# Normalizing the first twelve tiles on ScalarE and reading a wave of outputs back later, in a two-layer graph and expert network on one core

## The chip, the cores and the metric

One core of a Trainium2 chip runs the whole program in one launch. The core has TensorE (PE, matrix products; its weight loads are PEld), VectorE (DVE), ScalarE (ACT), GpSimd (POOL) and SyncE (SP), which here issues most of the transfers. The metric is the device time of one execution, in microseconds (us); lower is better.

## The reference, cut to what matters

3327 nodes have 256 features each. There are two layers, and each has a graph step and a step of eight experts, of which every node uses two.

```python
# layer 0
x = x + relu(adj @ (layernorm(x) @ W) + b)
x = x + moe0(layernorm(x))        # 8 experts, top 2, 256 -> 1024 -> 256, relu
# layer 1
a = tanh(adj * adj) where adj > 0  # top 700 of a row are kept
h2 = tanh(layernorm(x) @ W_proj + b_proj)
x = x + relu(a @ (h2 @ W_gcn) + b_gcn)
t = layernorm(x)
x = x + t + moe1(t)               # 8 experts, top 2, 256 -> 256 -> 256, gelu
```

`layernorm` subtracts a row's mean and divides by the root of its variance plus 1e-5. All is fp32.

## The kernel before

The nodes are padded to 3328, which gives 26 tiles of 128 rows. `x` holds all tiles in SBUF for the whole run, and `s` holds the right-hand operand of the graph product. The adjacency matrix comes in 13 panels of 256 columns, each in two chunks of 13 tiles (1664 KB); six ring buffers (`ring0` to `ring5`) take the chunks in turn, and the experts' weights later on. A tile framework records the program: it puts each instruction into the queue of its engine in a fixed order and sets the semaphore waits from the accesses it has recorded. `issue_after` and the helper `behind` move an instruction behind another one in that order.

**The start.** The loads of tokens and of the first chunk of panels 0 and 1 go out on SP in slices (line 147): for each of four groups of tiles, (0, 2), (2, 2), (4, 4) and (8, 5), the tokens, then panel 0's slice, then panel 1's; then the tokens of the last thirteen tiles. POOL meanwhile builds constants and issues six small transfers (`gnn_b_sb`, `f0_bg_sb`, `g1_wg_sb`, `f1_r_sb`, `f1_b1_sb`, `g1_bp_sb`; 1 to 256 KB). PE runs 54 short products on constants ahead of the first real one.

Line 1111 normalizes the tiles in groups: (0, 2), (2, 2), (4, 4), (8, 4), (12, 6), (18, 8). `statistics` (line 267) computes mean and variance on DVE, two instructions a tile, and the reciprocal root by three steps of Newton's method, in small dependent instructions. `layernorm` (line 290) then writes each tile of `s` with one DVE instruction, `(x - mean) * rs` (line 297). The first product, `aggregate_first` (line 371), takes the tiles j of the first chunk in order, and for each j first panel 0 and then panel 1 (line 424, `add`, line 383). Then it goes panel by panel. The bias `gnn_b_sb` is first read when panel 0 is finished (line 329). ScalarE counts the positive entries of each piece with Sign (line 1126); a ring buffer is loaded again when PE and these counts have read it.

**The end.** In layer 1 the experts work on blocks of tokens; `step` does one block. Its `second` (line 954) ends in `scatter` (line 551), an indirect transfer on POOL that writes the weighted outputs to rows of `ys1` in DRAM. The last six blocks hold 128 rows (one scatter), the others 256 (two). The outputs are read back from `ys1` with `load_outputs` (line 1050, issued by SP), added to `x` by `add_loaded` (line 1064, two DVE instructions for one read), and `x` is written to the result.

This read-back comes in three parts. Tiles 0 to 13 are the first wave: seven reads of two tiles (512 KB), one after each block from the 18th, each added two blocks later, with the write to the result (line 1384, ScalarE's queue) a block after that. Tiles 14 to 21 are the second wave: four reads of two tiles, after the 27th to the 30th of the 32 blocks. Tiles 22 to 25 are read one by one (256 KB) behind the last block. The loop adds only the first wave; the second one and the last four tiles are added in `with behind(last_y)` (line 1409), behind the last block's DVE work, and written by ScalarE's queue, two of them by SP's (line 1413). The list `written` holds the scatters that a wave must wait for; besides, the framework lets a read wait for the newest scatter that is recorded ahead of it. All loads of blocks are issued by SP ahead of the first read of the second wave.

Of the kernel before, what the change touches and what calls it, by code (L numbers as in the profile page):

```python
# [22 lines left out]
P = 128  # L23
NT = 26
# [67 lines left out]
def gnn_moe_two_layers(  # L92
# [41 lines left out]
    def piece(pan, k):  # L134
        return ring[(pan * NCHUNK + k) % RING].rearrange("p (c w) -> p c w", w=PW)
# [8 lines left out]
        gates.append(g)  # L144
        return d

    for t, n in [(0, 2), (2, 2), (4, 4), (8, CJ - 8), (CJ, NT - CJ)]:
        nc.sync.dma_start(out=x[:, t : t + n, :], in_=x_in[:, t : t + n, :])
        if t < CJ:
            for pan in range(2):  # L150
                nc.sync.dma_start(
                    out=piece(pan, 0)[:, t : t + n, :], in_=adjT[pan, 0, :, t : t + n, :]
                )

    ones_sq = const.tile([P, P], BF16, name="ones_sq")
    nc.gpsimd.memset(ones_sq, 1.0)
# [74 lines left out]
    def behind(instructions):  # L231

        if instructions and any(i is instructions[-1].ins for i in nc.cur_bb.bb.instructions):
            return tc.issue_after(instructions[-1].ins)
        return nullcontext()
# [7 lines left out]
    def on_all_partitions(name, b):  # L243
        t = const.tile([P, b.shape[1]], F32, name=name)
        nc.gpsimd.dma_start(out=t, in_=b.partition_broadcast(P))
        return t
# [3 lines left out]
        nc.gpsimd.dma_start(out=t, in_=a)  # L250
        return t

    gnn_b_sb = on_all_partitions("gnn_b_sb", g0_b[0:1, :])
    f0_bg_sb = on_all_partitions("f0_bg_sb", f0_bg[0:1, :])
    gate = state.tile([P, E, D], F32, name="gate")

# [114 lines left out]
    def aggregate_first(b_sb, w, w_sb, begin, count, after):  # L371

        sums, waiting, copied = {}, [], []

        def start(pan):
            sums[pan] = [psy.tile([P, PW], F32, name="ps_g", tag="py") for _ in range(DC)]

        def add(pan, j):
            for c in range(DC):
                nc.tensor.matmul(  # L383
                    sums[pan][c],
                    lhsT=s[:, j, ts(c, P)],
                    rhs=piece(pan, j // CJ)[:, j % CJ, :],
                    start=(j == 0),
                    stop=(j == NT - 1),
                )

        def finish():
            pan, g = waiting.pop()
            for it in range(PW // P):
                ps = psh.tile([P, D], F32, name="ps_o", tag="ph")
                for c in range(DC):
                    nc.tensor.matmul(  # L396
                        ps, lhsT=g[:, c, ts(it, P)], rhs=w_sb[:, c, :], start=(c == 0),
                        stop=(c == DC - 1),
                    )
                add_relu(x[:, pan * (PW // P) + it, :], ps, b_sb)  # L400
            after(pan)

        def rest(pan, first):
            for j in range(first, NT):
                add(pan, j)
                if waiting and j == first + BEHIND:
                    finish()
            g = work.tile([P, DC, PW], F32, name="xnT", bufs=2)
            for c in range(DC):
                copied.append(nc.scalar.copy(g[:, c, :], sums[pan][c]))  # L410
            waiting.append((pan, g))

        loaded = RING // NCHUNK
        for pan in range(loaded):
            load_panel(pan, lambda pan, k, a: None, begun=1 if pan < 2 else 0)
            if pan == 1:
                nc.sync.dma_start(out=w_sb, in_=w.rearrange("(c p) n -> p c n", p=P))
                with tc.issue_after(last_piece[0].ins):
                    turn_gate(f0_wgT)
        with tc.issue_after(last_piece[0].ins):  # L420
            turn_gate(f1_rT)
        for pan in range(2):
            start(pan)
        for j in range(CJ):
            for pan in range(2):
                add(pan, j)
        for pan in range(NPAN):
            if pan > 1:
                start(pan)
            if loaded < min(pan + RING // NCHUNK, NPAN):  # L430
                load_panel(loaded, lambda pan, k, a: None)
                loaded += 1
            begin(pan)
            count(pan, copied)
            rest(pan, CJ if pan < 2 else 0)
        return finish
# [648 lines left out]
    def fill(*lists):  # L1085


        with tc.issue_after(last_piece[0].ins):
# [13 lines left out]
            for xlist in lists:  # L1102
                for e in range(E):
                    first = xlist[e * NP : e * NP + SB, :].rearrange("(g p) d -> p g d", p=P)
                    nc.sync.dma_start(out=first[:, :, 0:ID], in_=zeros)
                    with nc.allow_non_contiguous_dma("two elements of a partition"):
                        nc.sync.dma_start(
                            out=first[:, :, ID : ID + 1], in_=rows_f[:, e, :].unsqueeze(2)
                        )

    for t0, n0 in [(0, 2), (2, 2), (4, 4), (8, 4), (12, 6), (18, 8)]:
        with behind(last_normalized if t0 < 12 else ()):
            layernorm(t0, n0, xn=s[:, t0 : t0 + n0, :].unsqueeze(2))

    with tc.issue_after(last_normalized[0].ins):
        g1_wg_sb = by_feature("g1_wg_sb", g1_wg)
        f1_r_sb = by_feature("f1_r_sb", f1_rT)
        f1_b1_sb = plain("f1_b1_sb", f1_b1)
        g1_bp_sb = plain("g1_bp_sb", g1_bp)

    def count(pan, copied):
        for k in range(NCHUNK):
# [225 lines left out]
    with tc.If(first_usual > 0) as arms:  # L1348
        output_loads.clear()
        for yt, t, n in begun:  # L1350
            load_outputs(yt, ys0, t, n, written, "read0")
        layer0.step(late)
        layer0.step(late)
        with behind(last_y):
            add_begun()
        layer0.step(late)
        with behind(last_y):
            statistics(0, BEGUN, begun_stats)
        layer0.steps_to(late, layer0.always)
        between()  # L1360
        layer1 = new_layer1()
        aggregate(gnn_b_sb, filter_chunk, panels1(layer1, True), loaded=ahead)
        late1 = first_blocks(layer1)

        layer1.steps_to(late1, EARLY - 1)
        layer1.step(late1, place=blk.tile([P, DC, SB], F32, name="xT_arms", bufs=1))
        baset, nbt = late1[4], late1[6]  # L1370
        second_usual = usual(
            [(FIRST_TILES, baset[:, E : 2 * E]), (MORE_TILES, baset[:, 2 * E :])],
            [(late1[5][0:1, :], FIXED[1])],
            nbt[:, E : 2 * E],
        )
        before_inner = layer1.state()
        with tc.If(second_usual > 0) as inner:  # L1377
            layer1.know(2 * E)
            waiting, asked, added, k = [], [], [], 0
            while len(layer1.started) < layer1.always:  # L1380
                layer1.step(late1)
                at = len(layer1.started)
                for tiles in added:
                    nc.scalar.dma_start(out=rows_of(out, *tiles), in_=x[:, tiles[0] : sum(tiles), :])
                added.clear()
                if at == EARLY + 2 * E - 2:
                    layer1.know_rest(late1)

                with behind(last_y):
                    if asked and asked[0][2] + 1 < at <= layer1.always - FIXED[1]:  # L1390
                        yt, tiles, _ = asked.pop(0)
                        add_loaded(yt, *tiles)
                        added.append(tiles)
                if waiting and at > waiting[0][1] + (1 if k < FIRST_TILES // 2 else 2):
                    tiles, _, written = waiting.pop(0)
                    yt = ring[k % RING][:, PIECE - 2 * K * D :].rearrange("p (n d) -> p n d", n=2)
                    load_outputs(yt, ys1, *tiles, written, "read1")
                    asked.append((yt, tiles, at))
                    k += 1
                if at in (EARLY + E, EARLY + 2 * E):  # L1400
                    tiles = range(0, FIRST_TILES, 2) if at == EARLY + E else range(FIRST_TILES, MORE_TILES, 2)
                    waiting.extend(((t, 2), at, list(outputs)) for t in tiles)
            assert not (waiting or added)
            left = []
            for i, t in enumerate(range(MORE_TILES, NT)):
                yt = ring[i][:, 0 : K * D].rearrange("p (n d) -> p n d", n=1)
                load_outputs(yt, ys1, t, 1, outputs)
                left.append((yt, (t, 1)))
            with behind(last_y):
                for i, (yt, tiles) in enumerate([(yt, tiles) for yt, tiles, _ in asked] + left):  # L1410
                    add_loaded(yt, *tiles)
                    queue = nc.sync if i > len(asked) and i % 2 else nc.scalar
                    queue.dma_start(out=rows_of(out, *tiles), in_=x[:, tiles[0] : sum(tiles), :])
        with inner.Else():
            layer1.back_to(before_inner)
            layer1.rest(late1)
            finish(FOURS)
# [168 lines left out]
```

## Time and profile before

| what | value |
|---|---|
| median of 4 runs | 1235.65 us |
| lowest and highest of them | 1230.36 and 1237.18 us |
| the profiled execution | 1230.29 us |
| its span in the profile | 1228.6 us |
| PE busy | 1188.8 us, 97% of the span |
| DVE, ACT, POOL busy | 707.4, 511.9 and 270.4 us |
| granted clock of PE | 0.994 of full speed |
| moved by DMA | 241.59 MB, mean 197 GB/s |

The span runs from the first to the last instruction of the profiled execution. A busy time is the sum of an engine's instructions; issuing a transfer and waiting are not in it. In the timeline a row gives the start and the duration in microseconds, the engine, the line, the operation, what it writes and reads, and in brackets how long its engine sat idle before it and what ended that. "x4" means four instructions in one row, whose duration then runs from the first one's start to the last one's end. SPq, ACTq and POOLq are the queues of those engines, in which transfers are issued. "L297" is line 297 of the kernel.

### The profile page before, as it was taken

To read this page: it belongs to the slowest core of one execution; us is meant where nothing else is said; L and a number is where in the kernel's file an instruction comes from. 1 tells how busy PE (TensorE), PEld (TensorE's weight loads), DVE (VectorE), ACT (ScalarE), POOL (GpSimd) and SP (SyncE) were. 2 spreads that over 40 slices of the span, in tenths; PEclk is the share of its full clock that TensorE was granted. 3 is DMA by queue.
4 is the path that set the end of the run, shared out by engine and by line. 5 is a ranking of instruction groups with operands and counts; after the bars stand their busy time and mean duration, and the time that the engine had idled before them with its cause. 6 is when DMAs were issued, how large, how long until landed. Compare 5 with 4: busy or idle time off the path is not lost. (4 is left out here: it accounts for less than half of the span.)

```text
span 1228.6 us, 18156 instructions
## 1 busy us (share of the span) xinstructions
PE 1188.8 (97%) x5819; PEld 1028.7 (84%) x5819; DVE 707.4 (58%) x2841; ACT 511.9 (42%) x950; POOL 270.4 (22%) x341
## 2 busy tenths in 40 slices
PE   8999999999999999999999999999999999988983
PEld 7888888888888888888888888888888888877872
DVE  7577756766682111211111268479999998776464
ACT  2655456445322222223232235995555552033331
POOL 3004111211241111111111110003224223254541
PEclk9999999999999999999999999999999999999997
DMA  9898744444357556757566647235445542476797
GB/s 340 192 325 259 207 160 154 159 159 138 102 189 251 181 184 188 251 180 252 185 219 224 245 171 286 75 149 201 173 147 195 184 152 79 136 232 186 230 295 229
DMA packets 123177, 241.59 MB, mean 197 GB/s; under 512 B 24480, under 2 KB 93120, under 8 KB 116160
## 3 DMA queue, kind: packets, MB, share of 16 engines
q1 hardware_dynamic: 108656, 205.59, 51.1%
q0 software_dynamic: 11136, 31.60, 7.0%
q10 hardware_dynamic: 3280, 3.15, 0.8%
q8 instruction: 48, 0.79, 0.3%
q14 instruction: 57, 0.47, 0.1%
HBM read 203.98 MB, written 36.33 MB: 196 GB/s over the span
## 5 line engine op out<-in xcount | busy, mean ns | idle before, releaser
L383 PE MATMUL ps_g<-ring,s 128*128 128x256 f32 x1352 | 295.6, 380 | 4.6 <-DVE s L297 4.6
L360 PE MATMUL ps_g<-s,ring 128*128 128x256 f32 x1352 | 294.2, 380 | 0.0
L383 PEld LDWEIGHTS ps_g<-ring,s 128*128 128x128 f32 x1352 | 255.7, 190 | 40.3 <-DVE s L297 6.0
L360 PEld LDWEIGHTS ps_g<-s,ring 128*128 128x128 f32 x1352 | 256.0, 190 | 34.4
L941 PE MATMUL ps_h<-xT,ring 128*128 128x256 f32 (+1 forms) x1176 | 249.3, 365 | 3.8 <-ACT xT L932 3.6
L941 PEld LDWEIGHTS ps_h<-xT,ring 128*128 128x128 f32 x1176 | 204.3, 190 | 41.1 <-ACT xT L932 4.7
L948 ACT ACTIVATE wide<-ps_h,ring 128x256 f32<-128x256 f32 (+1 forms) x240 | 110.3, 460 | 285.1 <-PE ps_h L941 264.8
L447 DVE SCALAR_TENSOR_TENSOR rt_product<-xn,gate 128x256 f32<-128x256 f32 x400 | 198.6, 497 | 12.2
L980 PE MATMUL ps_y<-ring,wide 128*128 128x256 f32 x896 | 200.3, 379 | 0.0
L551 POOL DMA_INDIRECT xlist<-xn,rt_idx x104 | 105.0, 1009 | 392.1 <-DVE ln_ve L278 154.4
L980 PEld LDWEIGHTS ps_y<-ring,wide 128*128 128x128 f32 x896 | 167.1, 190 | 21.0
L1126 ACT ACTIVATE sign<-ring,below 128x416 bf16<-128x416 f32 x208 | 133.5, 642 | 9.3 <-DMA ring<-in_adjT 3.1
L551 POOL DMA_INDIRECT ys<-narrow,index x56 | 54.9, 981 | 326.6 <-DVE narrow L988 234.6
L1275 ACT ACTIVATE ring<-ring 128x3328 f32<-128x3328 f32 x22 | 65.4, 2978 | 87.5 <-DVE ring L1274 50.7
L932 DVE COPY xT<-ptb 128x512 f32<-128x512 f32 (+1 forms) x29 | 18.9, 651 | 142.1 <-PE ptb L929 142.1
L987 DVE TENSOR_TENSOR narrow<-ps_y,ring 128x256 f32<-128x256 f32 x56 | 23.8, 424 | 131.7 <-PE ps_y L980 131.6
L512 ACT ACTIVATE rt_d<-rt_d 128x2 f32<-128x2 f32 x26 | 5.3, 203 | 162.9 <-DVE rt_d L511 162.2
L551 POOL DMA_INDIRECT ys<-wide,index x58 | 57.5, 991 | 62.5 <-DVE wide L988 34.1
L1276 ACT ACTIVATE ring<-ring 128x3328 f32<-128x3328 f32 x22 | 65.4, 2977 | 0.6
L329 DVE TENSOR_TENSOR gnn_t<-ps_o,gnn_b_sb 128x256 f32<-128x256 f32 x26 | 11.0, 424 | 82.8 <-PE ps_o L396 82.8
L980 PE MATMUL ps_y<-s,narrow 128*128 128x256 f32 (+1 forms) x200 | 48.4, 381 | 1.1 <-issue 1.0
L275 DVE BATCH_NORM_STATS2 ln_st<-x 128x6 f32<-128x256 f32 x104 | 42.1, 414 | 5.5 <-DMA x<-in_x 4.9
(213 smaller groups left out, 1035.1 us busy)
## 6 DMA issues: line engine op xcount, KB each, us to landing
ring<-in_adjT SPq DMA_DIRECT2D x50, 1664.0 KB
ring<-in_f_w1T SPq DMA_DIRECT2D x30, 1024.0 KB
ring<-in_f_w2T SPq DMA_DIRECT2D x30, 1024.0 KB
ring<-xlist SPq DMA_DIRECT2D x52, 258.0 KB
ring<-in_f_w SPq DMA_DIRECT2D x36, 256.0 KB
ring<-ys SPq DMA_DIRECT2D x12, 512.0 KB
ring<-in_f_b SPq DMA_DIRECT2D x34, 128.0 KB
xlist<-wide SPq DMA_DIRECT2D x16, 257.0 KB
```

The source lines that it names most:

```text
L275: nc.vector.bn_stats(out=st, in_=x[:, t0 + g, :])
L360: nc.tensor.matmul(ps[it], lhsT=chunks[k][:, c, ts(it, P)], rhs=s[:, j, :], start=(j == 0), stop=(j == NT - 1),)
L383: nc.tensor.matmul(sums[pan][c], lhsT=s[:, j, ts(c, P)], rhs=piece(pan, j // CJ)[:, j % CJ, :], start=(j == 0), stop=(j == NT - 1),)
L447: nc.vector.scalar_tensor_tensor(product, xn[:, g, 0, 0:D], 1.0, gate[:, e, :], ALU.mult, ALU.mult, accum_out=sc[:, g, e : e + 1],)
L551: d = nc.gpsimd.indirect_dma_start(out=a[:, :], out_offset=bass.IndirectOffsetOnAxis(ap=index, axis=0), in_=rows_, in_offset=None,)
L941: nc.tensor.matmul(ps, lhsT=w1[:, c, ts(hc, P)], rhs=xT[:, c, :], start=(c == 0), stop=(c == DC - 1),)
L948: nc.scalar.activation(hT[:, hc, :], ps, func, bias=bb1[:, hc : hc + 1])
L980: last_product[:] = [nc.tensor.matmul(ps, lhsT=hT[:, hc, ts(g, P)], rhs=w2[:, hc, :], start=(hc == 0), stop=(hc == hc_n - 1),)]
L987: nc.vector.tensor_tensor(y[:, g, :], ps, bb2, ALU.add)
L1126: nc.scalar.activation(sign, piece(pan, k)[:, :, ts(i, GROUP)], AF.Sign, bias=below, accum_out=positive[:, pan, i, k : k + 1],)
L1275: nc.scalar.activation(a, a, AF.Square)
L1276: nc.scalar.activation(a, a, AF.Tanh)
```

## The change

It has two halves.

In the first half, ScalarE writes `s` for tiles 0 to 11: DVE computes `shift = -mean * rs` for a group, one small instruction, and ScalarE then computes `Identity(rs * x + shift)` per tile, with `rs` and `shift` read from tiles. `behind(last_shift)` keeps each group's statistics behind the former group's shift on DVE. Tiles 12 to 25 are normalized on DVE as before. On SP the tokens of the second group go out ahead of panel 1's slice of the first group; the order of the other transfers there stays. Five of the six small transfers on POOL are made to follow the last normalization, and stand in POOL's queue behind the load of `gate` (line 258). The product takes the first chunk in pairs of tiles: tiles j and j + 1 for panel 0, then both for panel 1.

In the second half, the four reads of the second wave are recorded behind the loop over the blocks, ahead of the four single reads. Their list of scatters is the one of the same block as before. They are added and written where they were, in the same order; only the condition in the loop that kept them out of it is gone.

```diff
-    for t, n in [(0, 2), (2, 2), (4, 4), (8, CJ - 8), (CJ, NT - CJ)]:
+    def load_tokens(t, n):
         nc.sync.dma_start(out=x[:, t : t + n, :], in_=x_in[:, t : t + n, :])
-        if t < CJ:
-            for pan in range(2):
-                nc.sync.dma_start(
-                    out=piece(pan, 0)[:, t : t + n, :], in_=adjT[pan, 0, :, t : t + n, :]
-                )
+
+    def load_slice(pan, t, n):
+        nc.sync.dma_start(out=piece(pan, 0)[:, t : t + n, :], in_=adjT[pan, 0, :, t : t + n, :])
+
+    first_groups = [(0, 2), (2, 2), (4, 4), (8, CJ - 8), (CJ, NT - CJ)]
+    load_tokens(*first_groups[0])
+    for group, following in zip(first_groups, first_groups[1:]):
+        load_slice(0, *group)
+        if group[0] == 0:
+            load_tokens(*following)
+        load_slice(1, *group)
+        if group[0] > 0:
+            load_tokens(*following)
...
-        for j in range(CJ):
+        for j in range(0, CJ, 2):
             for pan in range(2):
-                add(pan, j)
+                for i in range(j, min(j + 2, CJ)):
+                    add(pan, i)
...
+    last_shift = []
     for t0, n0 in [(0, 2), (2, 2), (4, 4), (8, 4), (12, 6), (18, 8)]:
-        with behind(last_normalized if t0 < 12 else ()):
+        if t0 >= 12:
             layernorm(t0, n0, xn=s[:, t0 : t0 + n0, :].unsqueeze(2))
-
-    with tc.issue_after(last_normalized[0].ins):
-        g1_wg_sb = by_feature("g1_wg_sb", g1_wg)
-        ...
+            continue
+
+        with behind(last_shift):
+            mv, rs = statistics(t0, n0)
+            shift = work.tile([P, n0], F32, name="ln_shift")
+            last_shift[:] = [nc.vector.scalar_tensor_tensor(
+                shift, mv[:, :, 0], -1.0, rs, ALU.mult, ALU.mult
+            )]
+        for g in range(n0):
+            nc.scalar.activation(
+                s[:, t0 + g, :], x[:, t0 + g, :], AF.Identity, bias=shift[:, g : g + 1],
+                scale=rs[:, g : g + 1],
+            )
...
+    for t, w in [
+        (gnn_b_sb, g0_b[0:1, :].partition_broadcast(P)),
+        (g1_wg_sb, g1_wg.rearrange("(c p) n -> p c n", p=P)),
+        (f1_r_sb, f1_rT.rearrange("(c p) n -> p c n", p=P)),
+        (f1_b1_sb, f1_b1),
+        (g1_bp_sb, g1_bp),
+    ]:
+        follow(nc.gpsimd.dma_start(out=t, in_=w), last_normalized)
...
-                    if asked and asked[0][2] + 1 < at <= layer1.always - FIXED[1]:
+                    if asked and at > asked[0][2] + 1:
...
-                if waiting and at > waiting[0][1] + (1 if k < FIRST_TILES // 2 else 2):
+                if waiting and at > waiting[0][1] + 1:
...
-                if at in (EARLY + E, EARLY + 2 * E):
-                    tiles = range(0, FIRST_TILES, 2) if at == EARLY + E else range(FIRST_TILES, MORE_TILES, 2)
-                    waiting.extend(((t, 2), at, list(outputs)) for t in tiles)
-            assert not (waiting or added)
+                if at == EARLY + E:
+                    waiting.extend(((t, 2), at, list(outputs)) for t in range(0, FIRST_TILES, 2))
+                if at == EARLY + 2 * E:
+                    second_written = list(outputs)
+            assert not (waiting or added or asked)
+
             left = []
+            for t in range(FIRST_TILES, MORE_TILES, 2):
+                yt = ring[k % RING][:, PIECE - 2 * K * D :].rearrange("p (n d) -> p n d", n=2)
+                load_outputs(yt, ys1, t, 2, second_written, "read1")
+                left.append((yt, (t, 2)))
+                k += 1
             for i, t in enumerate(range(MORE_TILES, NT)):
                 ...
             with behind(last_y):
-                for i, (yt, tiles) in enumerate([(yt, tiles) for yt, tiles, _ in asked] + left):
+                for i, (yt, tiles) in enumerate(left):
                     add_loaded(yt, *tiles)
-                    queue = nc.sync if i > len(asked) and i % 2 else nc.scalar
+                    queue = nc.sync if tiles[0] >= MORE_TILES and i % 2 else nc.scalar
                     queue.dma_start(out=rows_of(out, *tiles), in_=x[:, tiles[0] : sum(tiles), :])
```

More of the change, by code (lines that the diff above doesn't have):

```diff
@@ L251, in plain @@
         return t
-    gnn_b_sb = on_all_partitions("gnn_b_sb", g0_b[0:1, :])
+    gnn_b_sb = const.tile([P, D], F32, name="gnn_b_sb")
     f0_bg_sb = on_all_partitions("f0_bg_sb", f0_bg[0:1, :])
@@ L1109, in fill @@
                         )
+    last_shift = []
     for t0, n0 in [(0, 2), (2, 2), (4, 4), (8, 4), (12, 6), (18, 8)]:
-        with behind(last_normalized if t0 < 12 else ()):
+        if t0 >= 12:
             layernorm(t0, n0, xn=s[:, t0 : t0 + n0, :].unsqueeze(2))
-    with tc.issue_after(last_normalized[0].ins):
-        g1_wg_sb = by_feature("g1_wg_sb", g1_wg)
-        f1_r_sb = by_feature("f1_r_sb", f1_rT)
-        f1_b1_sb = plain("f1_b1_sb", f1_b1)
-        g1_bp_sb = plain("g1_bp_sb", g1_bp)
+            continue
[10 more added lines that the diff above has]
+            )
+    g1_wg_sb = const.tile([P, DC, D], F32, name="g1_wg_sb")
+    f1_r_sb = const.tile([P, DC, E], F32, name="f1_r_sb")
+    f1_b1_sb = const.tile(list(f1_b1.shape), F32, name="f1_b1_sb")
+    g1_bp_sb = const.tile(list(g1_bp.shape), F32, name="g1_bp_sb")
+    for t, w in [
[6 more added lines that the diff above has]
+        follow(nc.gpsimd.dma_start(out=t, in_=w), last_normalized)
     def count(pan, copied):
```

## The prediction

> **What bounds the kernel now.** I read the busy table first, then PE's waits, then the timeline of the two ends of the span, because the table leaves nothing to win in between.
>
> ```profile
> PE 1188.8 (97%) x5819; PEld 1028.7 (84%) x5819; DVE 707.4 (58%) x2841; ACT 511.9 (42%) x950; POOL 270.4 (22%) x341
> ```
>
> PE is without work for only 40 us. Some 18.7 of them lie behind its last matmul (about 1209.9 of 1228.6). The largest wait in the list of PE's waits (engine, line, what it waited for; total, times, longest) is at the start:
>
> ```profile
> PE ps_g L383 <- DVE s L297: 4.6, 4, 1.7
> ```
>
> PE's timeline from 6 to 33 us (start, duration, what, idle before) shows the four places:
>
> ```profile
> 7.96 3.72 PE L383 MATMUL ps_g<-ring,s 128*128 128x256 f32 x16 [1.58 <-DVE s L297]
> 13.39 3.72 PE L383 MATMUL ps_g<-ring,s 128*128 128x256 f32 x16 [1.70 <-DVE s L297]
> 18.20 14.08 PE L383 MATMUL ps_g<-ring,s 128*128 128x256 f32 x64 [1.09 <-DVE s L297]
> 32.55 0.70 PE L383 MATMUL ps_g<-ring,s 128*128 128x256 f32 x2 [0.27 <-DVE s L297]
> ```
>
> From 32.55 PE runs without a gap into the next panels, so what counts is when tile 12 starts. The waits of DVE in the first 40 us, its timeline, and the DMA queues of that stretch (packets, MB, share of 16 engines) say what is behind it:
>
> ```profile
> DVE ln_st L275 <- DMA x<-in_x: 4.9, 3, 2.6
> 9.54 0.43 DVE L275 BATCH_NORM_STATS2 ln_st<-x 128x6 f32<-128x256 f32 x1 [1.31 <-DMA x<-in_x]
> 25.82 0.75 DVE L275 BATCH_NORM_STATS2 ln_st<-x 128x6 f32<-128x256 f32 x2 [0.99 <-DMA x<-in_x]
> 32.09 2.02 DVE L297 TENSOR_SCALAR s<-x,ln_mv,ln_guess 128x256 f32<-128x256 f32 x6
> q0 software_dynamic: 256, 0.42, 5.8%
> ```
>
> DVE waits for tokens of tiles 2-3 (until 9.54) and of tiles 13-25 (until 25.82); 6.27 us of statistics later tile 12 is normalized. POOL's transfers (q0) take 5.8% of 40 us, 2.3 us of all sixteen engines, inside the first 14 us.
>
> At the end, SP's, POOL's and DVE's timelines and the chain of waits (start, duration, what):
>
> ```profile
> 1204.66 0.38 SPq L1050 DMA_DIRECT2D ring<-ys  x1
> 1209.35 8.62 SPq L1050 DMA_DIRECT2D ring<-ys  x6
> 1206.73 0.97 POOL L551 DMA_INDIRECT ys<-wide,index  x1 [1.27 <-DVE index L962]
> 1211.07 1.17 POOL L551 DMA_INDIRECT ys<-wide,index  x1 [1.11 <-POOLq L1377]
> 1210.71 2.49 DVE L1064 TENSOR_TENSOR x<-x,ring 128x512 f32<-128x512 f32 x4
> 1213.78 0.69 DVE L1064 TENSOR_TENSOR x<-x,ring 128x512 f32<-128x512 f32 x1 [0.58 <-DMA ring<-ys]
> 1215.45 1.89 DVE L1064 TENSOR_TENSOR x<-x,ring 128x512 f32<-128x512 f32 x3 [0.99 <-DMA ring<-ys]
> 1222.98 0.88 DVE L1064 TENSOR_TENSOR x<-x,ring 128x256 f32<-128x256 f32 x2 [0.27 <-DMA ring<-ys]
> 1211.07 4.67 DMA ys<-wide,index
> 1217.58 5.31 DMA ring<-ys
> ```
>
> The reads of the second wave (four, 512 KB) go out at 1203.31, 1204.66, 1209.35 and about 1209.8. Their eight adds are done by 1217.34, while the chain waits for the last scatter (landed 1215.73) and the four last reads (256 KB, issued 1216.11 to 1217.58). The second wave is free now: it fills a wait.
>
> **The change, part by part: the start.** DVE loses 12 normalizing instructions (0.40 us each) and gains four shifts of 0.16 us. ScalarE gets twelve activations. No row shows one that reads the scale from a tile; the nearest are L948 (128x256, 0.46 us) below and the sign (128x416, 0.64 us) above. I take 0.5, nearer the row of equal size. The Trainium skill ("ScalarE: Activation LUTs", What ACT_TABLE_LOAD costs) speaks against ScalarE here: 186 ns and 0.833 ns an element, and 93 ns for each pointer operand. An estimate by that page is 0.585 us a tile against DVE's measured 0.40; by it the sum would be 0.1 us later. The function table's load (1.28 us in the row of the sign) moves to the landing of the first tokens at 3.75 and ends near 5.0; the first shift is ready at 7.6, so 2.6 us cover it, and it would cost 1.28 without them.
>
> First group: shift until 7.6, activation until 8.2, PE at 8.25 instead of 7.96: 0.3 lost. Second group: its tokens are issued ahead of one 256 KB slice, and five of POOL's six early transfers (0.4 MB) are gone from beside them. They landed at 9.54; between 4 and 10 us only 160 to 270 GB/s moved, so I expect them between 6 and 8.1. DVE is free at 7.6. The chain from statistics to first normalization took 3.38 (9.54 to 12.92): shift at 11.2 to 11.7, PE at 11.9 to 12.4 instead of 13.39. The third group's chain took 4.16 (13.57 to 17.73): PE at 16.1 to 17.9 instead of 18.20. Eight tiles take 14.08: PE wants tile 12 at 30.2 to 32.0, not 32.28.
>
> DVE normalizes tile 12 still, 6.27 us behind its tokens' landing. These move up from 25.82 by what left the queues: 1.0 us if only 0.42 MB at 426 GB/s count, 2.3 if the engines' time does. So tile 12 is ready (6.27 and 0.46 behind) at 30.2 to 31.5. Both together start it at 30.3 to 32.0: a gain of 0.5 to 2.3. If the stream gains nothing, 0; a loss of the 0.3 is the bound above. I take **-1.5**.
>
> Queues: the last four of the twelve activations stand behind three signs, and these behind the slice that landed at 19.41. Three signs with their reads take 2.3 (19.41 to 21.7), the fourth group's shift comes near 20, PE wants tile 8 at about 23.5: covered by 1 us, and if the slice is late PE waits as long. The signs behind them slip by some 2 us; they free ring buffers whose loads go to panels 25 us ahead. POOL's five transfers move behind the gate load (40.05) and take 3.4 us of it; its next real work is at 57.68, and the first reader of the bias is DVE at 51.9, about 8 us behind the landing near 44. The matmul order in pairs of tiles asks for panel 1's slice 0.9 us later. These cost nothing.
>
> **The end.** In the built program SP and DVE hold the same instructions in the same order as before; what moves is a wait. Each read waits for the newest scatter recorded ahead of it. Formerly those were blocks 26 to 29; now all four reads are recorded behind the loop, and the first waits for the last scatter. Behind it on SP stand the other seven reads, and DVE waits for all.
>
> When does that scatter land? Scatters that the trace lets me bound: issued 1202.22, landed by 1204.66 (2.4); issued 1206.73, landed by 1209.8 (3.0); the one at 1204.48 released the read at 1209.35 (4.9), and the last took 4.67, both with re-reads in flight. With none in flight I take 2.9: first read at 1214.3 instead of 1216.11, so -1.8 (0 to -2.3).
>
> From that issue: a 512 KB read landed 3.6 to 4.4 us after issue in the blocks before (1193.27 to 1197.44); I take 3.9. DVE then needs four pairs of dependent adds, 1.42 each (1196 to 1199 shows 0.72 from add to add), and four of 0.89: 9.3, sum 13.2. The transfers, 3.15 MB of reads and 1.05 MB of writes between them at the 0.38 to 0.41 MB/us of 1212 to 1214 and 1220 to 1222, take 10.2 to 11 after about 2 us of start, and the last add 0.9: 13.5. Formerly it was 7.75 (1216.11 to 1223.86). So +5.75, less 1.8: **+3.9**, between +2.5 and +6.
>
> The skill's "DMA: Bandwidth & Descriptors" (Anatomy of one DMA) gives 2.0 us and 436 KB a us, an estimate of 3.2 us for 512 KB; the trace's 3.6 to 4.4 disagrees. By the page the reads would be in by 9.2, DVE's chain (3.2 and 9.3) would decide, and the sum would be +3.0 instead of +3.9.
>
> **Sum.** -1.5 and +3.9: +2.4. The profiled execution took 1230.29 us (span 1228.6 and 1.7 around it): 1232.7. It lies 0.4% below the median of the runs, 1235.65, so there **1238.0**. A difference under 0.5% (6.2 us) can hardly be told from no change here.
>
> **Rivals.**
> - *The start gains nothing*: tile 12 stays bound to tokens that land at 25.8. For it: that transfer's place in SP's order is unchanged and the queues are full from 12 to 30 us. Against: 0.42 MB fewer lie ahead. +3.9: 1239.5.
> - *The tail is cheap*: scatter in 2.4, DVE's adds overlap as now (four in 2.49), start at its best. Against: add pairs are now dependent neighbours. -2.3 and +2.5: 1235.9, no change.
> - *Slower*: the burst does not reach 0.38 MB/us. The trace has 120 GB/s in 1216 to 1218 and 291 in 1218 to 1220, with writes among the reads. At 0.25, 4.2 MB take 16.8: sum 2 + 16.8 + 0.9 = 19.7, less 7.75 and 1.8: +10, with the start +8.6: 1244. It decides by 0.5% from a mean below about 0.29 MB/us.
> - *Faster*: the reads do not burden the end (the wait is released early) and the load phase moves up by all that PE waits, 4.6, plus 1.8 of scatter: 1229. The program's waits speak against it.
>
> **How the numbers follow.** Forecast 0.48; start gains nothing 0.20 (0.01 of it beyond 6.2); cheap tail 0.10; slower 0.15; faster 0.07. Same: 0.48 + 0.19 + 0.10 = 0.77; slower 0.16; faster 0.07. The range takes in forecast, idle start and cheap tail, with the terms' bounds (-2.3 + 2.5 to +0.3 + 6) and some 3 us by which the median of few runs wanders: 1232 to 1243.
>
> **What would show it.** Right: PE's gap before 13.4 gone and tile 12 starting 0.5 to 2.3 earlier; eight re-reads in one row on SP right behind the last scatter, that scatter landing in under 3.5, and 13 us from the first re-read to the last add. Wrong: second-wave reads issued before 1211 (shifted by the start), PE's wait at tile 12 grown by as much as the others shrank, or a last add less than 10 us behind the first read.

## The result, and the profile after

The changed kernel takes 1236.23 us (median of 44 runs), the kernel before 1233.76 us (71 runs). The ratio is 1.0023, with a 95% interval from 1.0015 to 1.003: 2.8 us slower, between 1.9 and 3.7. The forecast was +2.4, from -1.5 at the start and +3.9 at the end. The profiled execution of the changed kernel took 1236.94 us, its span is 1235.2 us.

The code has moved by some lines: the product is now L391 (L383 before), DVE's normalization L305 (L297), its statistics L283 (L275), the read-back L1059 (L1050), its add L1073 (L1064). ScalarE's normalization is L1133, the shift L1129.

The busy table has hardly moved: PE has the same 5819 products (its 4 us more are mostly stretches at a lower clock, see below), DVE has lost 4 us, ACT has gained 6.

```profile
PE 1192.8 (97%) x5819; PEld 1031.9 (84%) x5819; DVE 703.4 (57%) x2833; ACT 517.5 (42%) x962; POOL 270.0 (22%) x341
```

**The start.** The wait of PE (total, times, longest):

```profile
PE ps_g L391 <- ACT s L1133: 3.0, 2, 2.1
```

PE's timeline from 6 to 36 us:

```profile
7.91 7.36 PE L391 MATMUL ps_g<-ring,s 128*128 128x256 f32 x32 [0.90 <-ACT s L1133]
17.38 18.96 PE L391 MATMUL ps_g<-ring,s 128*128 128x256 f32 x79 [2.11 <-ACT s L1133]
```

Four gaps have become two. The gap of 1.70 ahead of the second group is gone: the first 32 products form one row. The gap ahead of the third group has grown from 1.09 to 2.11, and that group starts at 17.38 instead of 18.20. Behind it there is no gap any more, at tile 12 either. ScalarE's timeline of the same stretch shows what PE waits for:

```profile
3.67 1.28 ACT L1133 ACT_TABLE_LOAD   x1 [3.67 <-DMA x<-in_x]
7.26 1.09 ACT L1133 ACTIVATE s<-x,ln_shift,ln_guess 128x256 f32<-128x256 f32 x2 [2.30 <-DVE ln_shift L1129]
...
16.72 2.07 ACT L1133 ACTIVATE s<-x,ln_shift,ln_guess 128x256 f32<-128x256 f32 x4 [4.74 <-DVE ln_shift L1129]
```

Every group waits for its shift (the second by 2.55, the fourth by 0.34), that is for DVE's statistics; ScalarE itself is idle. The table load ends at 4.95 and is covered. DVE in turn waits for tokens, 7.3 us in all:

```profile
DVE ln_st L283 <- DMA x<-in_x: 7.3, 3, 3.3
```

Its timeline says for which:

```profile
7.32 0.75 DVE L283 BATCH_NORM_STATS2 ln_st<-x 128x6 f32<-128x256 f32 x2
12.36 0.75 DVE L283 BATCH_NORM_STATS2 ln_st<-x 128x6 f32<-128x256 f32 x2 [1.50 <-DMA x<-in_x]
24.61 0.75 DVE L283 BATCH_NORM_STATS2 ln_st<-x 128x6 f32<-128x256 f32 x2 [3.35 <-DMA x<-in_x]
30.89 2.02 DVE L305 TENSOR_SCALAR s<-x,ln_mv,ln_guess 128x256 f32<-128x256 f32 x6
```

The second group's tokens are there when DVE is free (7.32, no wait); they landed at 9.54 before. Those of the third group hold DVE up until 12.36, those of tiles 13 to 25 until 24.61 (25.82 before); with them end the statistics of the group that tile 12 belongs to.

What is left of this at the end of the first panel can be read from ScalarE's copy of panel 0's product, the first work behind the whole panel. It starts at 45.38 in the kernel before and at 45.66 in the changed one.

In this execution nothing is left. The busy times by stretch (window, its length, busy time and count of each engine, granted clock of PE, DMA share, GB/s) show where it went:

```profile
14.00:17.34 3.34, 1.27 (x6) 0.76 (x5) 2.89 (x17) 0.62 (x2) 0.00 (x0) 1.00 1.05 429
17.34:20.75 3.41, 3.37 (x8) 2.75 (x9) 2.99 (x20) 3.35 (x8) 0.00 (x0) 0.50 1.03 429
```

Behind the gap of 2.11 the granted clock is 0.50 for 3.41 us, in which PE gets through 8 products instead of 16 or 17: 1.7 us. The trace of before has no such stretch ahead of its idle tail.

**The end.** The chain of waits:

```profile
1213.73 2.41 DMA ys<-wide,index
1217.45 6.84 DMA ring<-ys
1224.35 5.04 DMA ring<-ys
```

SP's timeline, with the eight re-reads, and SP's waits for other re-reads (total, times, longest):

```profile
1216.26 8.41 SPq L1059 DMA_DIRECT2D ring<-ys  x8
SPq L1059 <- DMA ring<-ys: 4.0, 2, 2.7
```

DVE's timeline, with their sixteen adds:

```profile
1219.58 1.42 DVE L1073 TENSOR_TENSOR x<-x,ring 128x512 f32<-128x512 f32 x2 [6.13 <-DMA ring<-ys]
1222.61 1.42 DVE L1073 TENSOR_TENSOR x<-x,ring 128x512 f32<-128x512 f32 x2 [1.61 <-DMA ring<-ys]
1224.31 5.98 DVE L1073 TENSOR_TENSOR x<-x,ring 128x512 f32<-128x512 f32 x12 [0.29 <-DMA ring<-ys]
```

The busy times of the stretch from 2 us behind the first re-read to the landing of the last (as above):

```profile
1218.26:1229.39 11.13, 0.00 (x0) 0.00 (x0) 7.69 (x14) 0.00 (x0) 0.00 (x0) 0.50 1.01 342
```

All eight re-reads stand in one row, behind the last scatter, which lands in 2.41 instead of 4.67. They are not issued in one burst: the last two go out at 1222.65 and 1224.35, when the second and the third have landed, which is why the chain runs through two reads. The DMA engines are full all the same (share 1.01, 342 GB/s). The first add follows 3.3 us behind the first read, the last one ends at 1230.29, 14.0 behind it. From PE's last matmul (ends 1212.60) to the end of the span there are 22.6 us, 18.7 before.

### The profile page after: what moved, and what is told of

Same layout as the page of the kernel before. It is cut to its first block, busy times and chain, and to the rows that moved or that the text cites. A ratio compares the mean times of both kernels' runs of the same rounds, so it can differ in the third digit from the quotient of the medians.

```text
span 1235.2 us, 18165 instructions
## 1 busy us (share of the span) xinstructions
PE 1192.8 (97%) x5819; PEld 1031.9 (84%) x5819; DVE 703.4 (57%) x2833; ACT 517.5 (42%) x962; POOL 270.0 (22%) x341
## 5 line engine op out<-in xcount | busy, mean ns | idle before, releaser
L391 PE MATMUL ps_g<-ring,s 128*128 128x256 f32 x1352 | 296.9, 381 | 3.0 <-ACT s L1133 3.0
L391 PEld LDWEIGHTS ps_g<-ring,s 128*128 128x128 f32 x1352 | 256.9, 191 | 38.8 <-ACT s L1133 3.9
L283 DVE BATCH_NORM_STATS2 ln_st<-x 128x6 f32<-128x256 f32 x104 | 42.1, 414 | 8.0 <-DMA x<-in_x 7.3
```

The costliest lines, as they stand in the source:

```text
L283: nc.vector.bn_stats(out=st, in_=x[:, t0 + g, :])
L391: nc.tensor.matmul(sums[pan][c], lhsT=s[:, j, ts(c, P)], rhs=piece(pan, j // CJ)[:, j % CJ, :], start=(j == 0), stop=(j == NT - 1),)
```

## The experiments

All were compared with the kernel before on the same chip; medians differ between chips, so the ratios count. In each trace two lengths were read that don't depend on what happens in between: the start of the copy of panel 0, and the time from PE's last matmul to the end of the span.

| kernel | copy of panel 0 | last matmul to end | last scatter | us against before, 95% |
|---|---|---|---|---|
| before | 45.38 | 18.66 | 4.67 | |
| the whole change | 45.66 | 22.60 | 2.41 | +2.8 (+1.9 to +3.7) |
| e1_start_only | 44.30 | 18.40 | 3.70 | -3.1 (-5.1 to -1.0) |
| e2_end_only | 45.44 | 22.87 | 2.39 | +5.8 (+3.7 to +7.8) |
| e3_start_busy | 43.95 | 18.11 | 4.24 | -2.7 (-4.7 to -0.6) |
| e4_reads_early | 45.67 | 18.58 | 2.69 | -2.0 (-3.7 to -0.1) |
| e5_start_and_early | 43.64 | 17.14 | 3.08 | -2.7 (-4.2 to -1.2) |
| e6_pool_early | 44.53 | 18.75 | 4.83 | -2.3 (-4.1 to -0.6) |
| e7_dve_normalizes | 43.31 | 19.36 | 4.86 | +0.1 (-2.1 to +2.3) |
| e8_tokens_sooner | 43.33 | 17.99 | 3.35 | -3.2 (-4.7 to -1.7) |
| e9_sooner_on_dve | 43.25 | 19.12 | 4.30 | -2.9 (-4.3 to -1.7) |
| e10_two_late | 45.70 | 20.12 | 2.58 | -0.2 (-1.5 to +1.1) |

**The two halves apart.** `e1_start_only` is the changed kernel with the end of before, `e2_end_only` the kernel before with the changed end.

```diff
 e1_start_only, against the changed kernel
-                    if asked and at > asked[0][2] + 1:
+                    if asked and asked[0][2] + 1 < at <= layer1.always - FIXED[1]:
...
 e2_end_only, against the kernel before
-                    if asked and asked[0][2] + 1 < at <= layer1.always - FIXED[1]:
+                    if asked and at > asked[0][2] + 1:
...
```

> The first half of the change with the end of before. Theory (the start saves 1.4 us of waits, but PE's gap of 2.1 us ahead of tile 4 lets the granted clock fall to 0.5 for one window of 3.4 us, which costs 1.7): between -1.5 and +0.3 us against before, by how many executions lose the window; in the profile tile 12 is normalized near 30.9 instead of 32.1, and a stretch at half clock stands behind the gap. Rival (the start saves nothing, because tokens bind tile 12; the whole +2.5 us is the end's): 0 us and PE's first matmul of tile 12 at 32.5 at full clock throughout.

> The second half of the change with the start of before. Theory: +4 us (from the last matmul to the end of the span 22.6 us instead of 18.7), the last scatter lands in 2.4 us instead of 4.7, 14 us from the first read to the last add. Rival (the end costs only what the medians differ, the start nothing): +2.5 us.

The first half alone: 1233.35 us (12 runs) against 1236.27 (31), ratio 0.9975 (0.9959 to 0.9992). The second half alone: 1242.06 us (8 runs), ratio 1.0047 (1.003 to 1.0063). The signs are those of the forecast, and the two add up to +2.7, where the whole change has +2.8. The first half starts its products at 8.10, and its third group has this row in PE's timeline:

```profile
17.66 18.61 PE L391 MATMUL ps_g<-ring,s 128*128 128x256 f32 x85 [2.16 <-ACT s L1133]
```

Its stretch at the place where the whole change had half speed:

```profile
17.34:20.75 3.41, 3.09 (x14) 2.76 (x15) 3.06 (x18) 3.35 (x9) 0.00 (x0) 1.00 1.02 428
```

The same gap as in the whole change, and full clock behind it: now 1.1 us are left at panel 0. `e5_start_and_early` (below) has the same start once more, its third group at 17.00 and full clock, and there 1.7 us are left (43.64). The second half's trace has the old start. PE's timeline has this gap ahead of its second group:

```profile
13.67 22.67 PE L383 MATMUL ps_g<-ring,s 128*128 128x256 f32 x96 [2.26 <-DVE s L297]
```

and this stretch behind it:

```profile
13.82:17.23 3.41, 3.41 (x9) 2.66 (x10) 3.10 (x18) 0.00 (x0) 0.00 (x0) 0.50 1.03 413
```

So the half speed belongs to neither start: it follows either one in some executions. In the old start it costs panel 0 next to nothing (45.44 with it, 45.38 without), for it falls into time in which PE would have waited for the third group; in the new one no such wait is left behind it. The end is that of the whole change (scatter 2.39; from the first read, issued at 1222.88, to the first add 3.7 and to the end of the last 14.5).

**Is it the clock?** `e3_start_busy` is the first half with 18 short products on constants in PE's queue where the gap of 2.16 stood.

```diff
+            if j == 2:
+                busy = pst.tile([P, P], F32, name="ps_busy", tag="pt")
+                with tc.issue_after(last_add[0].ins):
+                    for _ in range(18):
+                        nc.tensor.matmul(busy, lhsT=ones_sq, rhs=ones_sq, start=True, stop=True)
```

> As the first half alone, with 18 products of 128x128 on constants (0.1 us each, 1.8 us) in PE's queue between tiles 3 and 4, in the gap. Theory (the clock falls for the gap): no stretch at half clock in the first 40 us, tile 12 starts near 31.4, and the time is 1 to 1.7 us below the first half alone, -1.5 us against before. Rival (the gap is harmless): the same time as the first half alone, or 0.3 more where PE reaches the filler late.

It took 1232.40 us (12 runs), ratio 0.9978 (0.9962 to 0.9995). PE's timeline:

```profile
15.25 1.17 PE L440 MATMUL ps_busy<-ones_sq 128*128 128x128 bf16 x18
17.31 19.05 PE L391 MATMUL ps_g<-ring,s 128*128 128x256 f32 x87 [0.90 <-ACT s L1138]
```

The gap shrinks to 0.90, panel 0 (43.95) lies between the two traces of that start without the filler (43.64 and 44.30), and the time is the same. On the mean over executions, half speed at the start costs less than these runs can tell; why the first half measures -3.1 and its trace shows -1.1 is not answered by it.

**The second wave the other way.** `e4_reads_early` is the kernel before with all four reads of the second wave recorded behind block 27, as soon as their rows are written; `e5_start_and_early` puts that on the first half.

```diff
-                if waiting and at > waiting[0][1] + (1 if k < FIRST_TILES // 2 else 2):
+                while waiting and at > waiting[0][1] + (1 if k < FIRST_TILES // 2 else 2):
...
                     k += 1
+                    if k <= FIRST_TILES // 2:
+                        break
```

> Before, with the four reads of the second wave all recorded behind block 27 (the program of before puts them behind blocks 27 to 30), so that they are done when the last scatter goes out. Theory (the last scatter's 4.7 us are contention with two of these reads): it lands in 2.4 to 3 us, the four single reads go out 1.7 to 2.3 us earlier, -2 us against before. Rival (4.7 us is the scatter's own time there): 0 us.

> The first half of the change with all four reads of the second wave recorded behind block 27 (no fillers). If the two parts add up: -3.1 and -2.0 give -5 us against before, with their intervals -2 to -8. Rival (the early reads only shift what the first half wins, since both shorten the same stream): no more than the first half alone, -3 us.

Early reads alone: 1235.22 us (12 runs), ratio 0.9984 (0.997 to 0.9999). With the first half: 1232.22 (11 runs) against 1234.82 (33), ratio 0.9978 (0.9966 to 0.999). In the first of these traces the scatter, issued at 1220.35, lands in 2.69, and the eight adds of the second wave run in one row of DVE's timeline beside it:

```profile
1219.98 4.90 DVE L1064 TENSOR_TENSOR x<-x,ring 128x512 f32<-128x512 f32 x8
```

The direction is the opposite of the change's: early reads gain or cost nothing, late ones cost some 4 us or more. The two gains don't add up (-3.1 and -2.0, together -2.7), so one of them is smaller than its middle value. The lengths at the end say which: over four traces with early reads (e4, e5, e8, e9) 17.1 to 19.1 us, mean 18.2; over five with the end of before (before, e1, e3, e6, e7) 18.1 to 19.4, mean 18.7. The ranges overlap; early reads are worth half a microsecond there or nothing. In `e4_reads_early` the 2.0 us that the scatter lands sooner are lost again behind it: from its landing to the last add 9.2 us pass (8.1 before), from there to the end 5.6 (4.7 before).

**The parts of the first half.** `e6_pool_early` leaves POOL's five transfers at their old place; `e7_dve_normalizes` lets DVE normalize the first twelve tiles; both are otherwise the first half alone.

```diff
 e6_pool_early
-        follow(nc.gpsimd.dma_start(out=t, in_=w), last_normalized)
+    gnn_b_sb = on_all_partitions("gnn_b_sb", g0_b[0:1, :])
...
 e7_dve_normalizes
-        if t0 >= 12:
+        with behind(last_normalized if t0 < 12 else ()):
             layernorm(t0, n0, xn=s[:, t0 : t0 + n0, :].unsqueeze(2))
...
```

> The first half alone, but POOL's five transfers stay where they were before, at 2 to 9 us. Theory (they hold back the tokens): tokens of tiles 4 to 7 land 0.7 to 1.2 us later than the 12.3 to 12.6 of the first half, those of tiles 13 to 25 near 25.8 instead of 23.6 to 24.6, tile 4 starts near 18.3, and 1 us or more of the gain is gone (-0.5 to -2 us against before). Rival (the order on SP and ScalarE do it): tile 4 starts near 17.4, -3 us as the first half alone.

> The first half alone, but with DVE normalizing the first twelve tiles as before. Theory (with the tokens in order DVE waits for them again, so that ScalarE's share is hidden): tile 4 starts within 0.5 us of the first half's 17.3 to 17.7, the first product 0.3 us earlier, and the time is that of the first half alone, -3 us. Rival (ScalarE is what saves): tile 4 starts at 18 or later and the gain is under 1 us.

POOL's transfers early: 1233.03 us (12 runs), ratio 0.9981 (0.9967 to 0.9995). DVE normalizing: 1234.78 us (12 runs), ratio 1.0001 (0.9983 to 1.0019). PE's timeline with POOL's transfers early:

```profile
13.11 3.72 PE L391 MATMUL ps_g<-ring,s 128*128 128x256 f32 x16 [1.29 <-ACT s L1133]
```

PE's timeline with DVE normalizing:

```profile
16.68 19.69 PE L391 MATMUL ps_g<-ring,s 128*128 128x256 f32 x90 [1.21 <-DVE s L305]
```

With POOL's transfers in the way the second group starts at 13.11, with a gap of 1.29; at panel 0 (44.53) that comes to 0.2 to 0.9 us against the two traces of the first half's start. DVE normalizing starts the third group at 16.68, a full microsecond sooner than ScalarE (17.66), and panel 0 (43.31) is 2.1 us earlier than in the kernel before, the best start of the runs up to then. And yet the time is that of before. Its 12 runs lie between 1229.84 and 1241.65, and its trace has half speed in four stretches from 1093 us on. Three readings are left: DVE's work at the start delays something that this trace doesn't show; stretches of half speed took the gain away; or chance, for the interval (-2.1 to +2.3) overlaps that of the first half (-5.1 to -1.0).

**Tokens sooner, and which engine normalizes.** `e8_tokens_sooner` is `e5_start_and_early` with the tokens of tiles 4 to 7 also ahead of a slice of panel 1. `e9_sooner_on_dve` is that with DVE normalizing, and was made to decide about the first of these readings.

```diff
-        if group[0] == 0:
+        if group[0] < 4:
             load_tokens(*following)
         load_slice(1, *group)
-        if group[0] > 0:
+        if group[0] >= 4:
             load_tokens(*following)
```

> As the first half with early reads, and the tokens of tiles 4 to 7 issued one place earlier on SP, ahead of panel 1's slice of tiles 2 and 3. Theory (tile 4 waits for these tokens alone): they land 0.6 to 1 us earlier, PE's gap ahead of tile 4 shrinks from 2.1 to about 1.3 us, and the time is 0.5 to 1 us below that of the kernel without this. Rival (tile 12 binds next, or the slice that is now later): the gap moves behind tile 3 or to tile 12, same time.

> The start of the change with the tokens of tiles 4 to 7 sooner and the second wave's reads early, but DVE normalizes the first twelve tiles. Theory (ScalarE's part earns nothing, and the missing gain of DVE's normalizing measured alone was the clock's spells of half speed): as fast as the same kernel with ScalarE, -3.2 us against before within some 1.5, with ScalarE's copy of panel 0 starting at 43.6 or earlier in the profile (45.38 before). Rival (DVE's normalizing gives its lead back later): within 1 us of before.

With ScalarE: 1231.85 us (11 runs) against 1234.82 (33), ratio 0.9974 (0.9962 to 0.9986). With DVE: 1221.92 us (12 runs) against 1225.11 (23), on a chip on which all kernels are quicker, ratio 0.9976 (0.9965 to 0.9986). PE's timeline with ScalarE:

```profile
16.21 14.08 PE L391 MATMUL ps_g<-ring,s 128*128 128x256 f32 x64 [0.63 <-ACT s L1133]
30.51 5.66 PE L391 MATMUL ps_g<-ring,s 128*128 128x256 f32 x25 [0.22 <-DVE s L305]
```

PE's timeline with DVE:

```profile
16.55 19.76 PE L391 MATMUL ps_g<-ring,s 128*128 128x256 f32 x90 [1.09 <-DVE s L305]
```

Both versions beat the kernel before by the same amount, and so, by the ratios, the changed one, and in both panel 0 is copied 2.1 us earlier (43.33 and 43.25). With `e8_tokens_sooner` the next wait is shown: at tile 12, for DVE's normalization (0.22). The rival (DVE's normalizing gives its lead back) wanted `e9_sooner_on_dve` within 1 us of before; its interval ends at -1.7. So who normalizes the first tiles is worth nothing that these runs can tell, to some 2 us, and by the traces the order of the transfers carries the start. What the sooner tokens add to `e5_start_and_early` (-2.7) they can't tell either. Half speed can be part of what `e7_dve_normalizes` lost: reckoned from the granted clock (as in "What stays open"), its runs had 28.0 us of it on the mean, those of `e6_pool_early` 25.0 and those of before on that chip 27.0. Whether that, and not chance, was the cause is not shown.

**A price for each late read?** `e10_two_late` is the kernel before with only the last two of the four reads behind the loop.

```diff
-                if waiting and at > waiting[0][1] + (1 if k < FIRST_TILES // 2 else 2):
+                if waiting and k < FIRST_TILES // 2 + 2 and at > waiting[0][1] + (1 if k < FIRST_TILES // 2 else 2):
...
             left = []
+            for tiles, _, written in waiting:
+                yt = ring[k % RING][:, PIECE - 2 * K * D :].rearrange("p (n d) -> p n d", n=2)
+                load_outputs(yt, ys1, *tiles, written, "read1")
+                left.append((yt, tiles))
+                k += 1
```

> The kernel before, with only the last two of the four reads of the second wave put behind the loop. Theory (the end is a fixed chain plus a price for each late read: scatter 2.4, first add 3.3 behind the first read, then 1.42 and 0.89 of DVE for each late pair and single): from first re-read to last add 3.3 + 2 x 1.42 + 4 x 0.89 = 9.7, or 10 by the bytes, against 7.75, less 1.8 to 2.3 of the scatter: 0 us against before, from -0.5 to +0.5. Rival (half of the reads late cost half of the +5.8 measured for four): +2.9.

It took 1225.17 us (12 runs) against 1225.11, ratio 0.9998 (0.9988 to 1.0009). The chain of waits and DVE's timeline:

```profile
1201.71 2.58 DMA ys<-wide,index
1204.30 5.25 DMA ring<-ys
```

```profile
1209.57 5.72 DVE L1064 TENSOR_TENSOR x<-x,ring 128x512 f32<-128x512 f32 x12 [5.74 <-DMA ring<-ys]
```

The first two reads are added from 1201.35 to 1203.84, while the last scatter is on its way, as before; the others take 11.0 us from the first late read (1204.30) to the last add (1215.29), against 9.7 to 10 by the sum. The scatter gives 2.1 back, and the runs show no difference; half of the price of four (+2.9) lies outside the interval. So the reads have no equal price each: the first two that are late are paid by the scatter's sooner landing, the next two by nothing, since the scatter has little left to gain (2.58 with two late, 2.41 with four). By the traces the end grows from 18.7 to 20.1 with two late and to 22.6 with four, where the runs allow no more than +1.1 for two.

## Why the prediction was right

**Sum.** -1.5 and +3.9 were forecast. For the start, the two traces that have it at full clock give -1.1 and -1.7 (`e1_start_only` and `e5_start_and_early`; the four traces with the start of before lie between 45.38 and 45.70). The end gives +3.94 (22.60 less 18.66). Together that is +2.2 to +2.8, and +2.8 was measured; in the changed kernel's own trace, with half speed in it, the start gives +0.3. "The start gains nothing" was wrong by these traces and by the run of the first half; "slower" and "faster" fell with the +3.94. That the sum fits so closely is also luck: by the runs of the halves the start is off by -1.6 and the end by +1.9, and the two cancel. The 1238.0 rested on a median of four runs, 1235.65; over 71 runs it is 1233.76. And the range's upper end is not the sum of its parts: 1235.65, 6.3 and 3 make 1245, not 1243.

**The first two groups.** Forecast: PE at 8.25, second group between 11.9 and 12.4. The traces have 7.91 and 8.10, and no gap at the second group. The activation was taken at 0.5; two take 1.09 and four 2.07, so 0.52 to 0.55 each. ScalarE waits for the shift in all four groups, so that these hundredths move PE by hundredths. The estimate from the Trainium skill ("ScalarE: Activation LUTs", What ACT_TABLE_LOAD costs), 0.585, holds for one activation by itself: the same section says that back-to-back ones overlap by about 93 ns, which makes an estimate of 1.08 for two and 2.06 for four, and the rows agree.

**The third group.** Forecast 16.1 to 17.9, seen 17.00, 17.38 and 17.66: the later half. The tokens of tiles 4 to 7, whose place in the queue has not changed, became the new wait (12.36, 1.50 of it waiting). Eight tiles from 17.00 to 17.66 put tile 12 at 31.08 to 31.74, a gain of 0.8 to 1.5: the 1.5 that was taken is the upper end of what the traces show. `e8_tokens_sooner`, which moves those tokens, starts at 16.21.

**Tile 12.** The tokens of tiles 13 to 25, with which its group's statistics end, landed 1.2 earlier (forecast 1.0 to 2.3; 1.9 and 2.5 in `e1_start_only` and `e5_start_and_early`) and it was ready in time: PE has no wait there. Table load and signs cost nothing that the traces show, as forecast; taking POOL's transfers back costs 0.2 to 0.9 at panel 0.

**The end.** Here too errors cancelled, two of 0.5 to 0.7. The first read starts 3.66 us behind the last matmul, 6.17 before: -2.5 instead of -1.8 (scatter 2.41, taken 2.9). From there to the last add it takes 14.0 against 7.75: +6.3 instead of +5.75. DVE's own chain (9.3) does not decide: its rows show waits of 1.61 and 0.29 for reads, and the last read lands 13.1 us behind the first one's issue. The rate was the mis-sized term: behind the first 2 us the engines, full, moved 0.34 MB/us, where 0.38 to 0.41 had been taken; fewer bytes (3.8 MB instead of 4.2) made up for most of it. That SP holds back the last two reads was not foreseen; with full engines it shows no cost of its own. The sum by the Trainium skill's figures ("DMA: Bandwidth & Descriptors", Anatomy of one DMA), all reads in by 9.2 and +3.0, was too low; the first landed within 3.3, near the page's 3.2. That section gives the figures for transfers that GpSimd issues, and SP issues these.

**What was missed.** The clock. The forecast reckoned gaps at their length, and a gap of 2.1 us can cost another 1.7 us behind it, by an estimate 0.8 on the mean (last section).

**What stays open.** The halves alone measure -3.1 and +5.8, their traces show -1.4 (1.1 at the start and 0.3 at the end) and +4.2 at most; the intervals reach these, but both miss on the outer side. The granted clock of the runs leans the same way: the time at half speed (twice the missing share of the clock, times the span) is 26.4 us on the mean in the runs of before, 24.4 with the first half alone, 34.1 with the second half alone, of which its longer idle tail explains 4 us (each mean is uncertain by some 1 us). Where PE is the limit, a stretch at half speed costs half its length: 2.0 us less would be worth 1.0 and 3.7 us more 1.9, an estimate that brings -1.4 to -2.4 and +4.2 to +6.1. Why the second half alone should meet more of it is not known.

## What to carry to other kernels

A wait that is taken away at the start hands over to the next transfer in the queue: ask which tokens are late next, and move those too (`e8_tokens_sooner`), before moving arithmetic to another engine. Reads that fill the wait for a last scatter are free; behind it they cost their transfer, less what the scatter gains by their absence, so that two of four moved for nothing and all four cost 4 us. A gap of PE is reckoned at its length plus what a lower clock behind it may cost. Where two halves of a change have opposite signs and sums of one or two microseconds, only a run of each half by itself shows that there is something to keep.

## What the runs showed of the hardware

**Half speed behind short gaps.** The granted clock dropped to 0.50 for 3.41 us behind a gap of 2.11 (the whole change) and 2.26 (`e2_end_only`), and in `e4_reads_early` behind one of 1.90. PE's timeline and the stretch of that trace:

```profile
13.35 19.22 PE L383 MATMUL ps_g<-ring,s 128*128 128x256 f32 x80 [1.90 <-DVE s L297]
```

```profile
14.00:17.41 3.41, 3.41 (x10) 2.70 (x9) 3.03 (x18) 0.00 (x0) 0.00 (x0) 0.50 1.01 410
```

Behind the gap of 2.16 in `e1_start_only` it did not, nor behind that of 1.85 in `e5_start_and_early`. The traces show what decides. Such stretches lie on a fixed raster: in each of the ten traces that have more than one, they begin whole multiples of 3.413 us apart. In `e7_dve_normalizes` they begin at 1093.08, 1103.32, 1175.00, 1198.89 and 1212.55, which is 3, 21, 7 and 4 times 3.413. What counts is how long PE was busy in the raster's window ahead. These are the windows ahead of the third group in the whole change, ahead of the stretch just shown in `e4_reads_early` (half speed followed both), and in `e5_start_and_early` (full clock followed):

```profile
13.92:17.34 3.42, 1.35 (x7) 0.84 (x5) 2.97 (x18) 0.62 (x2) 0.00 (x0) 1.00 1.05 430
10.59:14.00 3.41, 1.51 (x7) 1.01 (x7) 2.99 (x16) 0.00 (x0) 0.00 (x0) 1.00 1.05 376
13.73:17.14 3.41, 1.56 (x8) 1.05 (x7) 2.96 (x18) 0.79 (x2) 0.00 (x0) 1.00 1.04 427
```

Laid over all twelve traces, the raster gives 4235 windows at full clock. All 33 in which PE was busy for less than 0.40 were followed by half speed, 3 of the 24 between 0.42 and 0.53, and none of the others. So the same gap costs 1.7 us more when it empties one window, and nothing more when the raster cuts it in two. An estimate from these figures: a gap of 2.11 us leaves a window under 0.42 in some 45% of its positions on the raster, which is 0.8 us on the mean. The Trainium skill ("TensorE: Matmul & The Clock Gate", Part 1) describes a free-running window of 3.41 us, which these stretches confirm. Its rule against gaps of more than about 3.4 us is too generous for these traces, where 1.90 was enough.

**A scatter's landing.** The last 128-row scatter landed in 2.4 us where no re-read and no write of a result ran beside it (the whole change, `e2_end_only`), and in 3.7 to 4.9 in the five traces with the end of before; there two 512 KB re-reads go out ahead of it, by 1.2 and 1.7 us in the trace of before. Where the re-reads had gone out 5 us and more ahead, it took 2.58, 2.69, 3.08, 3.35 and, in `e9_sooner_on_dve`, 4.30: when a read was issued is not enough to tell. How full the DMA engines are tells more. Their share in the 2.4 us from the scatter's issue stands last but one in these rows (the clock ahead of it, GB/s behind), of the kernel before and of the whole change:

```profile
1211.07:1213.47 2.40, 0.00 (x0) 0.00 (x0) 2.13 (x4) 0.00 (x0) 1.17 (x1) 1.00 0.98 373
1213.73:1216.13 2.40, 0.00 (x0) 0.00 (x0) 0.00 (x0) 0.00 (x0) 0.97 (x1) 0.85 0.21 68
```

It is 0.17 to 0.21 in the four traces in which the scatter landed within 2.7 us, 0.40 and 0.58 where it took 3.35 and 3.08, and 0.71 to 1.05 in five of the six where it took 3.7 or more. The sixth is `e3_start_busy` (0.45 and 4.24), where a re-read goes out 0.2 us behind the scatter. No run varies this share alone.
